# An attention kernel on one core: the next image's v loaded by halves over 26 steps, the sum's halves added first, the output multiplied and stored sooner

## The chip, the core and the metric

The kernel runs on one core of a Trainium2 chip. The metric is the time of one execution on the device in microseconds. Five engines take part: TensorE (PE, with its weight loads shown as PEld), VectorE (DVE), ScalarE (ACT), GpSimd (POOL) and SyncE (SP). Here POOL and SP mostly issue transfers (DMAs). An instruction of an engine, and a transfer of a queue, waits until everything in front of it in the program order of that engine has been issued.

## What is computed

For each of four images of 64 x 64 positions with 256 channels: three projections, attention of all 4096 positions over all 4096, and a residual.

```python
q = jnp.einsum('bwhc,cd->bwhd', x, Wq) + bq
k = jnp.einsum('bwhc,cd->bwhd', x, Wk) + bk
v = jnp.einsum('bwhc,cd->bwhd', x, Wv) + bv
pq, pk, pv = q.reshape(B, -1, N), k.reshape(B, -1, N), v.reshape(B, -1, N)
energy = jnp.einsum('bcn,bcm->bnm', pq, pk)
attention = jax.nn.softmax(energy, axis=-1)
out = jnp.einsum('bcm,bnm->bcn', pv, attention).reshape(B, W, H, C)
return gamma * out + x
```

All is float32. The kernel gets that precision from faster matmuls by splitting each factor into a high part and rests, so that one product is made of three.

## The kernel before

**Steps.** The main loop (line 694) has B * STEPS = 4 * 128 = 512 steps. An image has 8 groups of 512 queries (`g`), a group 16 units of 256 keys (`t`, the unit's number in the group, `n % 16`). Step n does, for each engine in the order written out in the loop: `cross(n + 2)` and `energy(n + 2)` (TensorE: the scores of two steps ahead, lines 369 and 384; ScalarE: a scaling, line 370, and the exponential, line 387), `attend(n, 0)` and `attend(n, 1)` (TensorE: v times the exponentials, line 443, into PSUM banks `a` and `b` that collect over a group), `upper` (ScalarE, line 393) and `halves(n + 1)` (VectorE: adds the exponentials to the group's sum `s`, line 404, and makes the two other parts `l` and `d` of the split, lines 419 and 421, which `attend` of the next step reads).

**The next image's projections** are worked into the steps of the image before (`step`): two blocks of 256 positions per 16 steps, on top of the work above. Their q, k and v parts are stored to DRAM by `store` on SP's queue (line 338). For the last image's steps, from 384 on, there are none.

**Loads on POOL's queue**, in this order within a step: the keys of step n + 5 (`load_k`, line 356; three buffers, so it waits until `energy(n + 2)` has read the buffer), the q of the next group (`load_q`, line 350, in step t = 8), the v of the next image (`load_v`, line 343), and the accumulating load of `finish` (line 502). All of v stands in one tile, `vall[:, t, i]`, whose unit t is overwritten for the next image when the last group of this image is done with it. Before the change unit t of image c is loaded in step 128 c - 13 + t, both halves i in a row, so within 16 steps.

**The end of a group.** In step t = 15, `emptied(n, 0)` (ScalarE, line 463) writes the first half of the result from PSUM into the tile `o`, of which there is one; in step t = 0 of the next group `emptied(n - 1, 1)` writes the other half on VectorE (line 461). Before it may write, the group before must have been stored from `o`. The next group's `attend` needs the emptied banks. `finish` then does the rest of the group in pieces. It is a generator, and `proceed()` at the end of each step runs it to its next `yield`. Counting its pieces from k = 0 at the end of step t = 15, piece k runs in step t = k - 1 of the next group:

- k = 0: the sums `s` (128 x 1024, two halves) are written to DRAM, `zd` (line 469, SP).
- k = 1: they are read back regrouped into `y` (line 474, SP), a tile that shares its buffer with the q of every second group.
- k = 4: both parts of the result are added (line 480, VectorE).
- k = 7: `y` is reduced, transposed, reduced and inverted (lines 483 to 491, VectorE) and written to DRAM, `rd` (line 492, SP).
- k = 8: `rd` is read back to all partitions as `r` (line 495, SP).
- k = 10: the result is multiplied by `r` (line 498, VectorE).
- k = 11: x is added to it by an accumulating load (line 502, POOL).
- k = 14: the result is stored (line 505, SP).

The last group of all goes through `finish_last`, which adds the two halves of the sum in `whole` (line 410) before.

Of the kernel before, what the change touches and what calls it, by code (L numbers as in the profile page):

```python
# [9 lines left out]
F32 = mybir.dt.float32  # L10
# [3 lines left out]
ALU = mybir.AluOpType  # L14
AX = mybir.AxisListType
# [5 lines left out]
def kernel(  # L21
# [36 lines left out]
    nc = tc.nc  # L58
    B, W, H, C = x.shape
    P = 128  # L60
# [21 lines left out]
    NB = 512  # L82
    NJ = NB // P
    NG = N // NB
    NU = NM // 2
    STEPS = NG * NU
# [14 lines left out]
    with ExitStack() as fast:  # L101
# [8 lines left out]
        dram = pool("dram", 2, space=DRAM)  # L110
# [4 lines left out]

        vall = qkv.tile([P, NU, 2, 3, C], F32R, tag="v", name="v")
        wf = qkv.tile([P, 2, 3, KC, C], F32R, tag="wf", name="wf")
        zd = dram.tile([B * NG, 2, P, NB], F32, tag="zd", name="zd", bufs=1)
        rd = dram.tile([B * NG, NB], F32, tag="rd", name="rd", bufs=1)
        xs4 = work.tile([P, 4, 2, XB], F32, tag="o", name="xs", bufs=1)  # L120
        raw = ppool.tile([P, 2, KC, C], F32, tag="x", name="raw")
# [23 lines left out]
        qd, kf, vf, units, loads, now = {}, {}, {}, {}, {}, {}  # L145
# [35 lines left out]
        def image(b):  # L181
            for g in range(NG):
                qd[b, g] = dram.tile([P, NJ, 3, P], F32, tag=f"qd{g}", name=f"qd_{b}_{g}")
            for t in range(NU):
                kf[b, t] = dram.tile([P, 2, 3, P], F32, tag=f"kf{t}", name=f"kf_{b}_{t}")
                vf[b, t] = dram.tile([P, 2, 3, C], F32, tag=f"vf{t}", name=f"vf_{b}_{t}")
# [13 lines left out]
        def load_x(b, i):  # L200
            if b == B or i >= NI:
                return
            if b == 0:
                t = xs4[:, i % 4]
                if i:
                    nc.sync.dma_start(t, xv[b, i])
                loads["x", b, i] = t
                return
            pair = work.tile([P, 2, 2, XB], F32, tag="xd", name=f"x_{b}_{i}", bufs=1)
            for u in range(2):  # L210
                nc.sync.dma_start(pair[:, u], xv[b, i + u])
                loads["x", b, i + u] = pair[:, u]
# [125 lines left out]
                    nc.sync.dma_start(to, f.bitcast(F32))  # L338
            stores.clear()

        def load_v(b, t):
            for i in range(2):
                nc.gpsimd.dma_start(vall[:, t, i], vf[b, t][:, i])  # L343

        def q_tile(g, name, dtype=F32R):
            return work.tile([P, NJ, 3, P], dtype, tag=f"q{g % 2}", name=name, bufs=1)
# [16 lines left out]
        def cross(n):  # L363

            if n >= B * STEPS:
                return
            for i in range(2):
                e = units["e", n, i] = ps_e.tile([P, NB], F32, tag="e", name=f"e_{n}_{i}")
                nc.tensor.matmul(e, *forms(n, i, 2), start=True, stop=False, skip_group_check=True)  # L369
                nc.scalar.mul(e, e, -REST)  # L370
# [25 lines left out]
        def halves(n):  # L396
            if n >= B * STEPS:
                return
            x, h = units[n]

            def summed():
                if n % NU:
                    s = now["s"]
                    nc.vector.tensor_tensor(s, s, x, ALU.add)  # L404
                else:
                    now["s"] = x

            def whole():
                s = now["sum"] = now["s"]
                nc.vector.tensor_tensor(s[:, 0, :], s[:, 0, :], s[:, 1, :], ALU.add)  # L410

            after = 0 < n < 5
            if not after:
                summed()
            if n == B * STEPS - 1:
                whole()
            ld = ppool.tile([P, 2, 2, NB], F32R, tag="ld", name=f"ld_{n}")
            l, d = ld[:, 0], ld[:, 1]
            nc.vector.tensor_tensor(l, x, h.bitcast(F32), ALU.subtract)  # L419

            nc.vector.scalar_tensor_tensor(  # L421
                d, h.bitcast(F32), 1.0 + E, x, ALU.mult, ALU.subtract
            )
            if n == 2:
                next(vs)
                next(vs, None)
            if after:
                summed()
            units[n] = h, l, d
# [35 lines left out]
        def finish(n, o, s):  # L465
            b, g = divmod(n, NG)
            r4 = rall[:, n, :]
            for i in range(2):
                nc.sync.dma_start(zd[n, i], s[:, i, :])
            yield  # L470
            y = q_tile(n, f"y_{n}", F32).rearrange("p j f a -> p (j f) a")
            for j in range(NJ):
                for i in range(2):
                    nc.sync.dma_start(
                        y[j * 32 : (j + 1) * 32, NJ * i : NJ * (i + 1)],
                        zd[n, i].rearrange("(a p) (j c) -> j p a c", p=32, j=NJ)[j],
                    )
            for _ in range(3):
                yield
            nc.vector.tensor_tensor(o[:, 0], o[:, 0], o[:, 1], ALU.add)  # L480
            for _ in range(3):
                yield
            nc.vector.tensor_reduce(
                y[:, 8].rearrange("p (f c) -> p c f", f=NJ),
                y[:, :8].rearrange("p a (c f) -> p c f a", f=NJ),
                AX.X,
                ALU.add,
            )
            nc.vector.transpose(y[:, 9], y[:, 8])
            nc.vector.tensor_reduce(r4, y[:, 9].rearrange("p (f c) -> p f c", f=NJ), AX.X, ALU.add)  # L490
            nc.vector.reciprocal(r4, r4)
            nc.sync.dma_start(rd[n, :].rearrange("(p j) -> p j", j=NJ), r4)
            yield
            r = o[:, 1, 0]
            nc.sync.dma_start(r, rd[n, :].partition_broadcast(P))
            yield
            yield
            nc.vector.tensor_tensor(
                o[:, 0], o[:, 0], r.unsqueeze(1).to_broadcast([P, 2, NB]), ALU.mult
            )  # L500
            yield
            nc.gpsimd.dma_start(o[:, 0], xg[b, g], accum_op=ALU.add)
            for _ in range(3):
                yield
            nc.sync.dma_start(og[b, g], o[:, 0])

        def inside(ok, r):
# [186 lines left out]
        for n in range(B * STEPS):  # L694
            b, u = divmod(n, STEPS)
            g, t = divmod(u, NU)
            final = n == B * STEPS - 1
            if n == 0:
                image(1)
                load_x(1, 0)  # L700
            if u == STEPS - 5 and b + 2 < B:
                image(b + 2)
            if n == B * STEPS - 6:
                xr = ppool.tile([P, 2, NB], F32, tag="s", name="xr")
                nc.sync.dma_start(xr, xg[b, g])
            cross(n + LOOK)
            turn = t == NU - 1 and not final
            if t == 0 and n:
                upper(n + LOOK - 1)
            p = n - 2 + (n > 17)  # L710
            step(p, "act")
            late = n >= (B - 1) * STEPS
            if not final:
                attend(n, 0)
            if late and 1 <= t <= 2 and n > 1:
                emptied(n - 1 - t, 1, done, t - 1)
            energy(n + LOOK)
            load_k(n + LOOK + 3)
            store()
            if t == 0 and n:  # L720
                done = full
            if turn:
                emptied(n, 0)
            else:
                upper(n + LOOK)
            step(p, "pe")
            if turn:
                active.append(finish(n // NU, now["o"], now["s"]))
            if t == 0 and n and not late:
                emptied(n - 1, 1, done, vector=True)  # L730
            halves(n + 1)
            step(p, "dve")
            if final:
                finish_last(n, xr)
                break
            attend(n, 1)
            full = now["a", 1], now["b", 1]
            if n == 17:
                for engine in ("act", "pe", "dve"):
                    step(p + 1, engine)  # L740
            if t == 8 and n + NU < B * STEPS:
                load_q(*divmod(n // NU + 1, NG))
            if n >= STEPS - NU + 3 and (n - 3) // NU % NG == NG - 1 and (n - 3) // STEPS + 1 < B:
                load_v((n - 3) // STEPS + 1, (n - 3) % NU)
            proceed()

    NB = 512
    NG = N // NB
    NJ = NB // P
    NP = NM // 2  # L750
    with tc.If(nc.values_load(again[0:1, 0:1]) > 0), ExitStack() as general:
# [91 lines left out]
        for b in range(B):  # L843
# [16 lines left out]
            for g in range(NG):  # L860
                ps = []
                mx = work.tile([P, 2, NB], F32, tag="mx", name=f"gmx_{b}_{g}")
                for t in range(NP):
# [9 lines left out]
                    p = ppool.tile([P, 2, NB], F32, tag="p", name=f"gp_{b}_{g}_{t}")  # L873
# [52 lines left out]
                r = work.tile([P, NB], F32, tag="r", name=f"gr_{b}_{g}")  # L926
                nc.vector.reciprocal(r, zb)
                for s in range(2):
                    y = work.tile([P, NB], F32, tag="y", name=f"gy_{b}_{g}_{s}")
# [33 lines left out]
```

## Time and profile before

| | |
|---|---|
| median of 3 runs | 2329.9 us (2328.8 to 2330.72) |
| the profiled execution | 2329.92 us |
| its span in the profile | 2328.0 us |
| TensorE's granted clock | 0.999 |

A row of the busy table gives an engine's busy time, its share of the span and the number of instructions. A row of the waits reads "engine line <- what ended the wait: us in total, times, longest us". A row of the chain or of the timeline starts with the start and the duration in us; xN are N instructions merged, and a bracket gives the idle time before and what ended it. A row of instruction groups ends with busy us, mean ns of one, and idle time before. A row of a window gives its length, then busy us of PE, PEld, DVE, ACT and POOL with their counts of instructions, then TensorE's clock, the share of the DMA engines and GB/s. The rows of transfers give the size in KB and the median us from issue to landing; "DMA to landing" gives shortest, median and longest.

### The profile page before, as it was taken

The numbers are of one execution on the slowest core, as the hardware profiler recorded it, in microseconds if no ns is written. First come the engines' busy times: TensorE is split into PE (matmuls) and PEld (weight loads), VectorE is DVE, ScalarE is ACT, GpSimd is POOL, SyncE is SP. The second block draws the span as 40 slices with busy tenths as digits, with TensorE's granted clock in tenths as the row PEclk, the third lists the DMA queues.
The fourth block names the chain that finished last, engine by engine and source line by source line (L and its number), as shares of the span: only waits on it lengthen the run. The fifth ranks groups of instructions, "written<-read, shape, count | busy, mean of one in ns | idle before, by whom it ended". The sixth has DMA issues, their size and how long they took to land.

```text
span 2328.0 us, 31989 instructions
## 1 busy us (share of the span) xinstructions
PE 2309.8 (99%) x10758; PEld 1934.2 (83%) x10758; DVE 2175.0 (93%) x2174; ACT 1797.0 (77%) x2917; POOL 417.3 (18%) x716
## 2 busy tenths in 40 slices
PE   9999999999999999999999999999999999999998
PEld 9888888888878888888888888888887888888887
DVE  8999999999999999999999999999999999888988
ACT  7778777787777777777777777777787788788875
POOL 7111111111321111111132111111113111111110
PEclk9999999999999999999999999999999999999999
DMA  8567765577985776666698567665579745545553
GB/s 266 162 168 210 205 177 155 168 208 200 298 249 167 208 203 180 166 168 195 201 319 246 167 188 206 198 167 167 169 226 332 206 135 142 146 133 149 154 151 97
DMA packets 232190, 445.30 MB, mean 191 GB/s; under 512 B 27986, under 2 KB 109652, under 8 KB 232020
## 3 DMA queue, kind: packets, MB, share of 16 engines
q0 software_dynamic: 101120, 280.54, 45.0%
q1 hardware_dynamic: 130352, 162.38, 20.9%
q8 instruction: 88, 1.44, 0.3%
q14 instruction: 82, 0.67, 0.1%
q10 hardware_dynamic: 548, 0.26, 0.0%
HBM read 321.92 MB, written 120.39 MB: 190 GB/s over the span
## 4 chain that ended last, share of the span: by engine, by line
PE 96%; DMA 3%; ACT 0%; DVE 0%; issue 0%; POOL 0%; ACTq 0%; DVEq 0%
PE a L443 39%; PE e L384 19%; PE b L443 19%; PE e L369 10%; PE qv L257 5%; PE v L274 3%; PE xt L219 1%; DMA out_dram<-o 1%; DMA o<-in_x_dram 1%; DMA k<-kf 1%; DMA rows<-in_L_conv_bk_dram 0%; ACT qv L292 0%; POOL v L343 0%; ACT o L463 0%; POOL k L356 0%
## 5 line engine op out<-in xcount | busy, mean ns | idle before, releaser
L387 ACT ACTIVATE x<-e 128x512 f32<-128x512 f32 x960 | 522.1, 596 | 323.2 <-PE e L384 323.1
L370 ACT ACTIVATE e<-e 128x512 f32<-128x512 f32 x1024 | 546.4, 571 | 135.3 <-PE e L369 135.3
L443 PE MATMUL a<-h,v 128*128 128x512 f32 x2048 | 634.6, 391 | 4.6 <-ACT o L463 4.6
L443 PE MATMUL a<-ld,v 128*128 128x512 f32 x2048 | 631.7, 390 | 0.0
L443 PE MATMUL b<-ld,v 128*128 128x512 f32 x2048 | 631.6, 390 | 0.0
L419 DVE TENSOR_TENSOR ld<-x,h 128x1024 fp32r<-128x1024 f32 x480 | 586.1, 1221 | 37.0 <-ACT h L393 21.0
L404 DVE TENSOR_TENSOR s<-s,x 128x1024 f32<-128x1024 f32 x480 | 585.6, 1220 | 35.2 <-ACT x L387 34.0
L356 POOL DMA_DIRECT2D k<-kf x512 | 272.4, 532 | 1847.9 <-PE e L384 1753.1
L421 DVE SCALAR_TENSOR_TENSOR ld<-h,x 128x1024 fp32r<-128x1024 f32 x480 | 585.6, 1220 | 0.0
L384 PE MATMUL e<-q,k 128*128 128x512 f32 x2048 | 548.1, 390 | 0.0
L393 ACT ACTIVATE h<-x 128x1024 fp32r<-128x1024 f32 x480 | 510.6, 1064 | 14.2
L443 PEld LDWEIGHTS a<-ld,v 128*128 128x128 f32 x2048 | 384.8, 188 | 80.3
L443 PEld LDWEIGHTS b<-ld,v 128*128 128x128 f32 x2048 | 384.7, 188 | 80.0 <-DVE ld L421 0.2
L384 PEld LDWEIGHTS e<-q,k 128*128 128x128 f32 x2048 | 384.6, 188 | 79.4
L443 PEld LDWEIGHTS a<-h,v 128*128 128x128 f32 x2048 | 379.8, 188 | 79.3 <-ACT o L463 5.5
L369 PE MATMUL e<-q,k 128*128 128x512 f32 x1024 | 316.2, 390 | 2.5 <-DMA k<-kf 2.5
L369 PEld LDWEIGHTS e<-q,k 128*128 128x128 f32 x1024 | 191.7, 188 | 43.3 <-ACT o L463 1.8
L310 DVE SCALAR_TENSOR_TENSOR f<-f,qv 128x512 fp32r<-128x512 f32 x128 | 86.1, 683 | 0.3
L419 DVE TENSOR_TENSOR ld<-s,h 128x1024 fp32r<-128x1024 f32 x32 | 39.2, 1226 | 46.6 <-ACT h L393 46.6
L257 PE MATMUL qv<-wf,xf 128*128 128x256 f32 x576 | 78.2, 287 | 0.2
L257 PEld LDWEIGHTS qv<-wf,xf 128*128 128x128 f32 x576 | 74.7, 193 | 3.1 <-issue 0.9
L165 DVE SCALAR_TENSOR_TENSOR vf<-vf,v 128x512 fp32r<-128x512 f32 x96 | 65.4, 682 | 0.5 <-ACT vf L155 0.4
(88 smaller groups left out, 1129.2 us busy)
## 6 DMA issues: line engine op xcount, KB each, us to landing
k<-kf POOLq DMA_DIRECT2D x512, 384.0 KB, 3.6
vf<-vf SPq DMA_DIRECT2D x96, 384.0 KB, 5.2
v<-vf POOLq DMA_DIRECT2D x96, 384.0 KB, 8.3
kf<-f SPq DMA_DIRECT2D x128, 192.0 KB, 3.6
qd<-f SPq DMA_DIRECT2D x124, 192.0 KB, 3.8
q<-qd POOLq DMA_DIRECT2D x31, 768.0 KB, 6.2
zd<-s SPq DMA_DIRECT2D x62, 256.0 KB, 4.9
y<-zd SPq DMA_DIRECT2D x248, 64.0 KB, 4.4
```

What stands on the lines that cost most here:

```text
L257: nc.tensor.matmul(to[:, s, :], left, right.rearrange("p s a -> p (s a)") if w else right, start=(f == 2 and s == k == 0), stop=(f == 1 an ...
L310: nc.vector.scalar_tensor_tensor(f[:, :, :, j, :], h.bitcast(F32), s, y, ALU.mult, op)
L356: nc.gpsimd.dma_start(t, kf[b, u % NU])
L369: nc.tensor.matmul(e, *forms(n, i, 2), start=True, stop=False, skip_group_check=True)
L370: nc.scalar.mul(e, e, -REST)
L384: nc.tensor.matmul(e, *forms(n, i, f), start=False, stop=(f == 1), skip_group_check=True)
L387: nc.scalar.activation(x[:, i, :], e, AF.Exp, scale=(1.0 + E) ** 3 / E)
L393: nc.scalar.activation(h, units[n], AF.Identity, scale=UPPER)
L404: nc.vector.tensor_tensor(s, s, x, ALU.add)
L419: nc.vector.tensor_tensor(l, x, h.bitcast(F32), ALU.subtract)
L421: nc.vector.scalar_tensor_tensor(d, h.bitcast(F32), 1.0 + E, x, ALU.mult, ALU.subtract)
L443: nc.tensor.matmul(to, vall[:, t, i, f, j * P : (j + 1) * P], units[n][f][:, i, :], start=(t == 0 and i == 0 and f != 1), stop=(t == NU - ...
```

## The change

Four parts:

- `load_v` loads one half of a unit. The 32 halves m = 0 to 31 for image c are issued in steps 128 c - 13 + 13 m // 16, so in 26 steps (128 c - 13 to 128 c + 12), one or two halves a step. They reach into the first 13 steps of image c, where unit t is used from step 128 c + t on.
- At the end of each group, not only of the last, `whole` adds the second half of the sum to the first on VectorE, in step t = 14, before `l` and `d` of that step. `zd` gets one half (one write instead of two), `y` is read with four transfers instead of eight, and the first reduction goes over 512 instead of 1024 elements per partition.
- One `yield` less before the multiplication: it and the accumulating load are one unit sooner (k = 9 and k = 10).
- One more `yield` less before the store: it is two units sooner (k = 12).

```diff
-        zd = dram.tile([B * NG, 2, P, NB], F32, tag="zd", name="zd", bufs=1)
+        zd = dram.tile([B * NG, P, NB], F32, tag="zd", name="zd", bufs=1)
...
-        def load_v(b, t):
-            for i in range(2):
-                nc.gpsimd.dma_start(vall[:, t, i], vf[b, t][:, i])
+        def load_v(b, t, i):
+            nc.gpsimd.dma_start(vall[:, t, i], vf[b, t][:, i])
...
-            if n == B * STEPS - 1:
+            if n % NU == NU - 1:
                 whole()
...
-            for i in range(2):
-                nc.sync.dma_start(zd[n, i], s[:, i, :])
+            nc.sync.dma_start(zd[n], s[:, 0, :])
             yield
             y = q_tile(n, f"y_{n}", F32).rearrange("p j f a -> p (j f) a")
             for j in range(NJ):
-                for i in range(2):
-                    nc.sync.dma_start(
-                        y[j * 32 : (j + 1) * 32, NJ * i : NJ * (i + 1)],
-                        zd[n, i].rearrange("(a p) (j c) -> j p a c", p=32, j=NJ)[j],
-                    )
+                nc.sync.dma_start(
+                    y[j * 32 : (j + 1) * 32, :NJ],
+                    zd[n].rearrange("(a p) (j c) -> j p a c", p=32, j=NJ)[j],
+                )
...
             nc.vector.tensor_reduce(
-                y[:, 8].rearrange("p (f c) -> p c f", f=NJ),
-                y[:, :8].rearrange("p a (c f) -> p c f a", f=NJ),
+                y[:, 4].rearrange("p (f c) -> p c f", f=NJ),
+                y[:, :NJ].rearrange("p a (c f) -> p c f a", f=NJ),
                 AX.X,
                 ALU.add,
             )
-            nc.vector.transpose(y[:, 9], y[:, 8])
-            nc.vector.tensor_reduce(r4, y[:, 9].rearrange("p (f c) -> p f c", f=NJ), AX.X, ALU.add)
+            nc.vector.transpose(y[:, 5], y[:, 4])
+            nc.vector.tensor_reduce(r4, y[:, 5].rearrange("p (f c) -> p f c", f=NJ), AX.X, ALU.add)
...
             nc.sync.dma_start(r, rd[n, :].partition_broadcast(P))
             yield
-            yield
             nc.vector.tensor_tensor(
                 o[:, 0], o[:, 0], r.unsqueeze(1).to_broadcast([P, 2, NB]), ALU.mult
             )
             yield
             nc.gpsimd.dma_start(o[:, 0], xg[b, g], accum_op=ALU.add)
-            for _ in range(3):
-                yield
+            yield
+            yield
             nc.sync.dma_start(og[b, g], o[:, 0])
...
-            if n >= STEPS - NU + 3 and (n - 3) // NU % NG == NG - 1 and (n - 3) // STEPS + 1 < B:
-                load_v((n - 3) // STEPS + 1, (n - 3) % NU)
+            for m in range(2 * NU):
+                c, r = divmod(n + NU - 3 - 13 * m // 16, STEPS)
+                if r == 0 and 0 < c < B:
+                    load_v(c, m // 2, m % 2)
             proceed()
```

## Prediction

> **What bounds the kernel now.** I read the busy table first, then the waits, then the chain that ended last, and only then single stretches.
>
> ```profile
> PE 2309.8 (99%) x10758; PEld 1934.2 (83%) x10758; DVE 2175.0 (93%) x2174; ACT 1797.0 (77%) x2917; POOL 417.3 (18%) x716
> ```
>
> The span is 2328.0 us, so TensorE is idle for 18.2 us of it. Something can be gained only inside that idle time, and most of it lies at the start and the end. The waits name what lies between:
>
> ```profile
> ACT o L463 <- DMA out_dram<-o: 5.4, 2, 3.1
> ...
> PE a L443 <- ACT o L463: 4.6, 2, 2.7
> PE e L369 <- DMA k<-kf: 2.5, 3, 1.4
> ```
>
> Two kinds of wait, five events, all where one image passes into the next. In two of them ScalarE (L463) cannot empty PSUM into `o`, because the store of the group before still reads `o`; attend (L443) then waits for the bank. In three, the keys of a coming step land late. The chain of waits shows the first kind around 640 us, and the pace beside it:
>
> ```profile
> 605.00 0.46 PE e L369 x2
> 605.46 0.91 PE a L443 x4
> ...
> 617.74 10.71 DMA o<-in_x_dram
> 628.45 0.02 issue
> 628.47 14.19 DMA out_dram<-o
> 642.66 0.02 issue
> ...
> 643.48 1.20 PE a L443 x4
> ...
> 1793.66 12.15 DMA k<-kf
> 1805.81 0.14 issue
> 1805.95 0.70 PE e L369 x2
> ```
>
> Read the middle lines as a relay: the accumulating load of x took 10.71 us, the store of the result followed it at once and took 14.19, and TensorE stood until it had landed. In the last lines a key load of 12.15 us does the same at the third boundary. Idle time understates the loss, because the first matmuls behind a wait are slower than usual: four cost 1.20 instead of 0.91 (+0.29, twice), two cost 0.70 instead of 0.46 (+0.24, three times). **The loss at the boundaries** is 4.6 + 2.5 + 0.6 + 0.7 = 8.4 us. Some 0.2 more goes in the matmuls that come next, which is an estimate; I take 8.6.
>
> Why are these transfers slow just there? Stretches of 16 us around the first boundary, and the same phases 32 steps (143.6 us) earlier, where no v is loaded (last columns: DMA share, GB/s). The distance is read from the chain, in which the same 16 projections stand 32 steps apart:
>
> ```profile
> 458.07 1.91 PE qv L257 x16
> 601.70 1.91 PE qv L257 x16
> ...
> 616.00:632.00 16.00, 16.00 (x72) 13.29 (x71) 15.50 (x16) 12.91 (x21) 7.57 (x13) 1.00 1.12 343
> 632.00:648.00 16.00, 13.33 (x59) 10.71 (x59) 10.57 (x11) 10.99 (x19) 4.78 (x9) 1.00 1.12 389
> ...
> 472.40:488.40 16.00, 16.00 (x72) 13.26 (x71) 15.48 (x16) 12.89 (x21) 3.28 (x5) 1.00 0.91 270
> 488.40:504.40 16.00, 16.00 (x76) 13.37 (x75) 13.68 (x14) 13.14 (x23) 2.12 (x4) 1.00 0.83 251
> ...
> 552.40:568.40 16.00, 16.00 (x73) 13.25 (x72) 13.47 (x15) 12.57 (x22) 2.12 (x4) 1.00 0.79 257
> ```
>
> The DMA engines are full (share 1.12) at 343 to 389 GB/s. The v loads fill them: the clock stays at 1.00 and nothing else differs. Key loads show the backlog, first from 600 to 660 us, then from 440 to 570 us:
>
> ```profile
> DMA to landing us min/median/max: 3.6/8.6/10.9
> ...
> DMA to landing us min/median/max: 3.3/3.6/5.9
> ```
>
> **The v loads over 26 steps.** The change issues the same 32 halves of 384 KB (0.393 MB) at each boundary, 12.6 MB, two POOL issues per unit as now; what moves is their time.
>
> ```profile
> v<-vf POOLq DMA_DIRECT2D x96, 384.0 KB, 8.3
> ```
>
> Sixteen steps last 71.8 us (half of 143.6), so v now asks for 175 GB/s; over 26 steps (116.7 us) it asks for 108. Added to the rows without v that is 270 + 108 = 378, 251 + 108 = 359 and, in the ten new steps behind the boundary, 257 + 108 = 365 GB/s, where the old demand was 270 + 175 = 445. From the second I take off 33, for half of the sum's write and reads (below). So the demand falls from well above 343 to 389 to just about that. At worst, (378 - 343) x 16 us = 0.56 MB queue up, 1.6 us of work at 343 GB/s; a key load then lands in 3.6 to 5.9 + 1.6, at most 7.5 us. What does it need?
>
> ```profile
> 608.02 0.53 POOL L356 DMA_DIRECT2D k<-kf  x1 [4.42 <-PE e L384]
> ...
> 612.10 0.53 POOL L356 DMA_DIRECT2D k<-kf  x1 [1.68 <-PE e L384]
> ```
>
> Steps without projections are 4.08 us apart; a key load starts 3.02 us into its step (605.00 above) and is used at the start of the third step after it: 3 x 4.08 - 3.02 = 9.2 us. So **the key waits go, 2.5 + 0.7 us**; the bound on the other side is a backlog as large as now, which leaves them (rival 1).
>
> A figure of the Trainium skill speaks against this. Its page DMA: Bandwidth & Descriptors, section Bandwidth, says that the HBM side binds HBM transfers at about 358 GB/s when both cores of a pair stream, and that all issuers share one set of 16 engines. By 358 the slice of 378 still backs up, by an estimated 0.3 MB or 1 us, which is inside the 1.6 above; the row of 389 already carried more than 358, so the row decides.
>
> The queue's new neighbours: POOL runs in order, so each half stands behind that step's key load and before the accumulating load. Instead of two issues a step (some 0.53 us each, like a key load's) there is mostly one, and no added wait: a unit is overwritten at least three steps after its last use, as the step numbers in the code show. The last half, of unit 15, is issued in step 12 of the new image, 3.02 + 0.53 us into it, and used 3 steps later at 0.46: 3 x 4.08 + 0.46 - 3.55 = 9.1 us of cover. Landings with both halves in each step and little else (585 to 600 us):
>
> ```profile
> DMA to landing us min/median/max: 3.8/4.3/4.6
> ```
>
> I take 5 to 7 us: no wait. The upper bound is in rival 4.
>
> **Multiplied, added and stored sooner.** At the boundary the store (L505) was issued in the instant in which the x load had landed (628.45, 628.47), so its place in the program did not hold it; only the multiplication one unit earlier does something there: at least 4.08 us for load and store alike. PE lost 2.67 + 0.29 there and less at the second boundary, so even with landings of 10.71 and 14.19 us this shift alone covers **both store waits, 4.6 + 0.6 us**. Two parts of the change thus cover the same 5.2 us; it counts once. The price is SP: two units sooner, the store waits at the head of SP's queue for the accumulating load, and the stores of q and k forms stand behind it. Usual landings (L502, then L505):
>
> ```profile
> DMA to landing us min/median/max: 6.1/6.5/12.0
> ...
> DMA to landing us min/median/max: 3.0/5.2/14.2
> ...
> 622.24 0.32 SPq L338 DMA_DIRECT2D kf<-f  x1
> ```
>
> The accumulating load now comes one step sooner, behind the key load of 612.10 and one half: 612.10 + 2 x 0.53 = 613.2. With 6.5 to 8 us to landing the store leaves SP at 619.7 to 621.2, before the next one there has its data (622.24). Price nothing; with 10.71 it leaves at 623.9, and the forms' stores wait 1.7 us. Those are needed only in the next image, or by a buffer some steps on.
>
> The multiplication must have `r` one unit sooner. In the group before the boundary:
>
> ```profile
> 603.12 0.34 SPq L495 DMA_DIRECT2D o<-rd  x1
> ...
> 608.95 1.22 DVE L404 TENSOR_TENSOR s<-s,x 128x1024 f32<-128x1024 f32 x1
> ...
> 611.22 1.22 DVE L421 SCALAR_TENSOR_TENSOR ld<-h,x 128x1024 fp32r<-128x1024 f32 x1
> ...
> 614.13 0.41 PEld L443 LDWEIGHTS b<-ld,v 128*128 128x128 f32 x2
> ...
> DMA to landing us min/median/max: 3.9/4.7/6.3
> ```
>
> The new place is 608.95, 5.83 us after `r` was issued; `r` takes 4.7 (last line), at most 6.3, which would hold VectorE 0.47 us. Behind it stands the splitting of the next step, whose L421 ends at 612.44 and is needed at 614.13: 1.69 us of cover, of which the multiplication itself (1.22, as every add of this size) leaves 0.47. Both ends are covered, so I take nothing.
>
> **The halves added first.** VectorE gets one 128x512 add per group, and the regrouping reduces 512 instead of 1024 elements:
>
> ```profile
> L410 DVE TENSOR_TENSOR s<-s 128x512 f32<-128x512 f32 x1 | 0.7, 694 | 0.0
> L483 DVE TENSOR_REDUCE y<-y 128x128 f32<-128x1024 f32 x31 | 61.9, 1995 | 0.0
> ...
> 273.59 1.23 DVE L419 TENSOR_TENSOR ld<-x,h 128x1024 fp32r<-128x1024 f32 x1 [0.80 <-PE e L369]
> ...
> 277.65 1.23 DVE L419 TENSOR_TENSOR ld<-s,h 128x1024 fp32r<-128x1024 f32 x1 [1.10 <-ACT h L393]
> ```
>
> The add costs 0.69 us in the step in which VectorE idles 0.80 and 1.10 us; if that cover were gone it would delay ld by 0.69. The shorter reduction is not in the trace: no saving at one end, half of 1.995 (1.0 us) at the other. I take 1.0, as adds go by length here (1.22 and 0.69). It lets `r` start 1 us sooner and pays for the add. One of two writes of the sum and four of eight reads go: 0.5 MB per group, 33 GB/s in a slice. None is on TensorE's path: nothing.
>
> **Sum**, against the profiled execution: 2329.92 us (span 2328.0 and 1.92 outside), which is the median of the three runs, 2329.9. Minus store waits 5.2, minus key waits 3.2, minus the slow matmuls behind 0.2: 2329.9 - 8.6 = **2321.3 us**. More is not there to gain, as the other idle time stands at the ends.
>
> **Rivals.**
> 1. *The keys take the store's place.* If the backlog stays, key loads wait at the first two boundaries too, 10.9 - 9.2 = 1.7 us each, or 3.2 as at the third. The loss is then 2 x 1.7 + 3.2 = 6.6 to 9.6 where it was 8.4, so 2328 to 2331. For it: key loads between 600 and 660 us took up to 10.9 and were hidden only because TensorE stood. Against it: the v demand falls by 67 GB/s. This is also the case in which the spreading does not do what it says.
> 2. *Only the store waits go*: 2329.9 - 5.2 = 2324.7. For it: the third boundary had no store wait and the longest key loads; against it, the groups behind that boundary have no projections and little other traffic.
> 3. *`r` holds VectorE, slower.* Place: the multiplication, in all 31 groups. `r` may take 5.83 + 0.47 = 6.3 us free; from 6.58 (8.6 / 31 = 0.28 more) the change loses. At 7.3 us it costs 31 x 1.0 = 31, so 2352. For it: 6.3 was seen; against it, the median is 4.7 and the shorter reduction starts it sooner.
> 4. *The last v halves come late, slower.* At the longest landing of keys, 12.15 us, against 9.1, they cost 3.05 us at three boundaries on top of rival 1: 2329.5 + 9.2 = 2339. Against it: one half a step.
>
> **How the numbers follow.** Forecast 78%, with its own range 2319.9 to 2323 (the runs before spread by 1 us each way; 1.5 for a remaining wait). Rival 1 has 8%, rival 2 7%, rival 3 4%, rival 4 3%. A measurement of this kernel tells about 0.2%, 4.7 us, from no change. Faster: the forecast and most of rival 2, 0.83; within: rival 1 and the rest of 2, 0.10; slower: 0.07. The range goes from 2319.9 to 2326.0, to take rival 2 in; about 15% is left out.
>
> **What would show it.** In the changed kernel the waits list should have no L463 on the store and no L369 on keys; key loads around the boundaries should land below 9 us, with a median near 5; v below 8. The reduction should be near 1.0 us; VectorE may wait for `r` some tenths. A wait of TensorE on keys or v in steps 0 to 15 of an image, or of DVE on `o<-rd` above 0.6 us in every group, would make the prediction wrong, and so would a new idle of TensorE in the step of the added half.

## The result, and the profile after

| | before | changed |
|---|---|---|
| median of 12 runs | 2329.9 us | 2324.4 us |
| single executions | 2326.8 to 2330.7 | 2321.6 to 2331.7 |
| the profiled execution | 2329.92 us | 2321.56 us |
| its span | 2328.0 us | 2319.7 us |

The ratio of the times is 0.9981, with a 95% interval from 0.9972 to 0.999. The change makes the kernel faster: by 4.4 us when the ratio is taken (2.3 to 6.5 by its interval), by 5.5 us when the medians are, where 8.6 were forecast. Two things stand out. The profiled execution is almost exactly at the forecast of 2321.3, but it is the fastest of the twelve. And the single executions of the changed kernel spread over 10 us where those of before spread over 4.

The waits of the changed kernel, in which L442, L368, L355 and L462 are the lines that were 443, 369, 356 and 463:

```profile
POOL k L355 <- PE e L383: 1799.5, 497, 5.5
...
ACT vf L155 <- DMA qd<-f: 9.6, 8, 2.4
...
DVE vf L165 <- ACT vf L155: 4.0, 6, 1.0
...
DVE o L494 <- DMA o<-rd: 2.7, 3, 1.3
...
PE e L368 <- ACT x L386: 0.3, 1, 0.3
```

The forecast waits are gone: no row has the emptying of the banks waiting for the store, and none has TensorE waiting for keys. In their place a row has grown that was small before: ScalarE, before the first operation on a v form (L155), waits until a store of an earlier q form (`qd<-f`) has landed and its buffer is free. Before the change the row was

```profile
ACT vf L155 <- DMA qd<-f: 2.7, 5, 0.9
```

The DMA engines around the first boundary, in the columns shown before (DMA share, GB/s):

```profile
616.00:632.00 16.00, 16.00 (x71) 12.86 (x70) 14.33 (x15) 12.13 (x20) 4.15 (x8) 1.00 1.10 355
632.00:648.00 16.00, 16.00 (x75) 12.92 (x74) 14.12 (x15) 13.21 (x23) 4.63 (x9) 1.00 1.08 344
680.00:696.00 16.00, 16.00 (x72) 13.25 (x71) 15.18 (x15) 12.55 (x20) 5.97 (x11) 1.00 1.01 300
```

In the first two of these stretches, 32 us long, they are still full, but the backlog is smaller. The key loads from 600 to 660 us (first line; 3.6/8.6/10.9 before) and all v halves (second; 3.7/8.3/13.9 before) land sooner:

```profile
DMA to landing us min/median/max: 3.3/5.8/8.6
...
DMA to landing us min/median/max: 3.7/5.9/10.2
```

The rows of the transfers show who pays (last number: median us from issue to landing). First two rows of before, then the changed kernel, whose accumulating load took 6.5 before:

```profile
kf<-f SPq DMA_DIRECT2D x128, 192.0 KB, 3.6
qd<-f SPq DMA_DIRECT2D x124, 192.0 KB, 3.8
...
kf<-f SPq DMA_DIRECT2D x128, 192.0 KB, 4.7
qd<-f SPq DMA_DIRECT2D x124, 192.0 KB, 5.4
...
o<-in_x_dram POOLq DMA_DIRECT2D x31, 512.0 KB, 7.5
```

These are medians over all groups, so the collision is not one of the boundaries alone. Away from the boundaries it is not waited for: there the latest landing on record of a first block's stores is 51.4 to 54.9 us into its group, and ScalarE takes the buffer at 55.5. All eight waits stand in the last group of an image or the first of the next, where v loads run too. Where it reaches TensorE can be followed in the timeline of the first steps of the second image (POOL, SP, ScalarE, TensorE):

```profile
684.60 1.15 POOL L498 DMA_DIRECT2D o<-in_x_dram  x1
...
686.12 0.32 SPq L338 DMA_DIRECT2D kf<-f  x1
686.49 0.77 SPq L338 DMA_DIRECT2D qd<-f  x1
687.31 0.97 SPq L338 DMA_DIRECT2D kf<-f  x1
688.32 1.22 SPq L338 DMA_DIRECT2D qd<-f  x1
693.62 0.60 SPq L501 DMA_DIRECT2D out_dram<-o  x1
...
697.85 0.60 ACT L155 ACTIVATE vf<-v 128x512 fp32r<-128x512 f32 x1 [2.38 <-DMA qd<-f]
698.35 1.08 ACT L386 ACTIVATE x<-e 128x512 f32<-128x512 f32 x2
...
698.99 0.99 PE L368 MATMUL e<-q,k 128*128 128x512 f32 x2 [0.32 <-ACT x L386]
```

The accumulating load leaves POOL 1.5 us before the first of the four stores of the first block's q and k forms leaves SP. The chain of waits has the last of them on it, issued at 688.32 and landing 9.42 us later:

```profile
688.32 9.42 DMA qd<-f
697.75 0.02 issue
```

ScalarE stands 2.38 us for it, the exponential behind it is late, the score bank is not free, and TensorE waits. Counted over step lengths (each step's length from the starts of its score matmuls, against the usual length of its place in the group), TensorE loses 1.7 us in this execution, where it lost 8.8 before: 0.5 in steps 125 and 127 ahead of the first boundary, 1.0 in steps 140 and 141 behind it, 0.1 in step 383.

The two rows of the sum, the regrouping's reduction and the added half:

```profile
L480 DVE TENSOR_REDUCE y<-y 128x128 f32<-128x512 f32 x31 | 33.3, 1074 | 0.0
L409 DVE TENSOR_TENSOR s<-s 128x512 f32<-128x512 f32 x32 | 22.2, 692 | 1.1
```

### The profile page after: what moved, and what is told of

Same layout as the page of the kernel before. It is cut to its first block, busy times and chain, and to the rows that moved or that the text cites. A ratio compares the mean times of both kernels' runs of the same rounds, so it can differ in the third digit from the quotient of the medians.

```text
span 2319.7 us, 31772 instructions
## 1 busy us (share of the span) xinstructions
PE 2308.2 (100%) x10758; PEld 1930.9 (83%) x10758; DVE 2169.7 (94%) x2205; ACT 1796.3 (77%) x2917; POOL 416.6 (18%) x716
## 4 chain that ended last, share of the span: by engine, by line
PE 98%; DMA 1%; DVE 0%; ACT 0%; issue 0%; SPq 0%; ACTq 0%; DVEq 0%
PE a L442 40%; PE e L383 20%; PE b L442 20%; PE e L368 10%; PE qv L257 5%; PE v L274 3%; PE xt L219 1%; DMA qd<-f 0%; DMA raw<-in_L_conv_Wk_dram 0%; SPq L338 0%; ACT qv L292 0%; ACT x L386 0%; DVE s L403 0%; DVE xf L165 0%; ACT h L392 0%
## 5 line engine op out<-in xcount | busy, mean ns | idle before, releaser
L442 PE MATMUL a<-h,v 128*128 128x512 f32 x2048 | 633.5, 390 | 0.0
L442 PE MATMUL a<-ld,v 128*128 128x512 f32 x2048 | 631.0, 389 | 0.0
L442 PE MATMUL b<-ld,v 128*128 128x512 f32 x2048 | 630.8, 389 | 0.0
L355 POOL DMA_DIRECT2D k<-kf x512 | 272.5, 532 | 1849.0 <-PE e L383 1799.5
L442 PEld LDWEIGHTS a<-ld,v 128*128 128x128 f32 x2048 | 384.5, 188 | 80.6
L442 PEld LDWEIGHTS b<-ld,v 128*128 128x128 f32 x2048 | 384.3, 188 | 80.3 <-DVE ld L420 0.2
L442 PEld LDWEIGHTS a<-h,v 128*128 128x128 f32 x2048 | 379.7, 188 | 74.1
L368 PE MATMUL e<-q,k 128*128 128x512 f32 x1024 | 316.3, 390 | 0.3 <-ACT x L386 0.3
L368 PEld LDWEIGHTS e<-q,k 128*128 128x128 f32 x1024 | 192.0, 188 | 41.4 <-ACT x L386 1.1
```

The lines of the kernel that those rows point to most:

```text
L355: nc.gpsimd.dma_start(t, kf[b, u % NU])
L442: nc.tensor.matmul(to, vall[:, t, i, f, j * P : (j + 1) * P], units[n][f][:, i, :], start=(t == 0 and i == 0 and f != 1), stop=(t == NU - ...
```

## The experiments

**Theory T**: the accumulating load, one unit sooner, falls among the stores of step t = 10; their buffer comes free late. **Rivals**: V, the v halves in the new steps 131 to 140 do it; S, the store of the result, two units sooner, stands at the head of SP's queue and holds the stores behind it; M, the multiplication one unit sooner disturbs VectorE.

"Loss" below is what TensorE loses by the step lengths of the profiled execution, counted as above. Parts are named A (v spread), B (halves added first), C (multiplication and accumulating load one unit sooner) and D (store one unit sooner still).

**A alone.** The kernel of before with

```diff
-        def load_v(b, t):
-            for i in range(2):
-                nc.gpsimd.dma_start(vall[:, t, i], vf[b, t][:, i])
+        def load_v(b, t, i):
+            nc.gpsimd.dma_start(vall[:, t, i], vf[b, t][:, i])
...
+            for m in range(2 * NU):
+                c, r = divmod(n + NU - 3 - 13 * m // 16, STEPS)
+                if r == 0 and 0 < c < B:
+                    load_v(c, m // 2, m % 2)
```

> Only the v loads spread over 26 steps; sum, multiplication and store as before. Theory T (the accumulating load, one unit sooner, lands among the stores of the first q and k forms in step t = 10, their buffer comes free late, ScalarE waits at the first v form and TensorE behind it): no such collision here, so all boundary waits of 8.4 us go and nothing is added: 2321 to 2323, narrow spread, ScalarE's wait on qd<-f near the 2.7 us of before. Rival V (the v halves in steps 131 to 140 themselves delay the forms' stores): 2324 and a spread of 5 us or more, wait on qd<-f about 9 us. If the store wait at the boundaries needs the sooner multiplication, L463 still waits and the time is 2325 to 2327.

Measured: 2320.0 us (2320.0 to 2322.1, 5 runs), ratio 0.9961 (0.9948 to 0.9975). TensorE loses 0.0 us over all steps, and the wait has gone:

```profile
ACT vf L155 <- DMA qd<-f: 0.2, 1, 0.2
```

So the spread alone takes all the boundary waits, store waits included, and its time lies below that of the whole change (and 1 us below what T expected). V falls.

**B, C and D without A.** The changed kernel with both places of the diff above undone.

> The change without the spread: v loaded in 16 steps as before, sum halved, multiplication and store sooner. The prediction's rival 1 as a kernel: store waits go (covered by one unit), key waits appear at all three boundaries, 6.6 to 9.6 us in all: 2328 to 2331. If the key waits do not appear at the first two boundaries: 2324.7. Theory T adds 1 to 3 us to either and a spread.

Measured: 2333.7 us (2332.2 to 2340.6, 11 runs), ratio 1.0023 (1.0014 to 1.0032), slower than before. No emptying waits for the store, so C and D (beside B) do cover the store waits without A; which of them does was not tried. But neither does TensorE wait for keys. What stands there is the same row as in the changed kernel, larger: 17.5 us in 6 waits over the whole run, and from 615 to 640 us these rows:

```profile
ACT vf L155 <- DMA qd<-f: 4.8, 2, 3.9
...
PE e L369 <- ACT x L387: 1.9, 1, 1.9
```

Step lengths give a loss of 13.7 us, all in steps t = 12 to 15 of the last groups of the first three images. The buffer of the forms is waited for before the key buffers are, although key loads took up to 10.4 us.

**A and B, without C and D.**

```diff
             nc.sync.dma_start(r, rd[n, :].partition_broadcast(P))
             yield
+            yield
...
             nc.gpsimd.dma_start(o[:, 0], xg[b, g], accum_op=ALU.add)
             yield
             yield
+            yield
             nc.sync.dma_start(og[b, g], o[:, 0])
```

> The change with multiplication, accumulating load and store back at k = 10, 11 and 14; v spread and sum halved. Theory T: 2321 to 2322.5, spread below 3 us, wait on qd<-f 3 us or less, no store wait at the boundaries. Rival V: 2324 and the spread of the changed kernel. Rival S (the store at the head of SP's queue delays the forms' stores): also 2321 to 2322.5, so this run does not tell S from T.

Measured: 2321.5 us (2320.3 to 2322.0, 5 runs), ratio 0.9965 (0.9951 to 0.9979), loss 0.0. ScalarE has no wait on `qd<-f` at all. B costs nothing on TensorE, and no step gets shorter either.

**A, B and C; the store at its old place, k = 14.**

```diff
             nc.gpsimd.dma_start(o[:, 0], xg[b, g], accum_op=ALU.add)
             yield
             yield
+            yield
+            yield
             nc.sync.dma_start(og[b, g], o[:, 0])
```

> The change with only the store's place back at k = 14; multiplication and accumulating load stay one unit sooner. Theory T: as the changed kernel, about 2324 with its spread, wait on qd<-f 7 us or more. Rival S: 2321 to 2322.5 and the wait on qd<-f down to 3 us.

Measured: 2322.3 us (2321.7 to 2325.4, 7 runs), ratio 0.997 (0.9959 to 0.9982). The wait stays, as T has it, and all five of its pieces (1.0 to 3.2 us) are at the first v form (t = 12):

```profile
ACT vf L155 <- DMA qd<-f: 8.5, 5, 3.2
```

TensorE loses 2.5 us. The time, however, is in the range that was expected for S (2321 to 2322.5) and not at the 2324 that was expected for T. So C accounts for a part only.

**The multiplication alone sooner** (A and B; multiplication at k = 9, accumulating load at k = 11, store at k = 14).

```diff
             yield
+            yield
             nc.gpsimd.dma_start(o[:, 0], xg[b, g], accum_op=ALU.add)
             yield
             yield
+            yield
             nc.sync.dma_start(og[b, g], o[:, 0])
```

> The change with the multiplication one unit sooner (k = 9) but the accumulating load back at k = 11 and the store at k = 14. Theory T (the accumulating load among the stores of the first forms is what costs): no TensorE loss, 2320 to 2321.5, wait of ScalarE on qd<-f below 1 us, forms' stores of step 10 near 4.1 us to landing. Rival M (the multiplication, in front of the next steps' work on VectorE or held by r, is what costs): 2322 to 2323 as with only the store put back, and the wait on qd<-f stays.

Measured: 2319.4 us (2319.3 to 2321.6, 5 runs), ratio 0.9961 (0.9947 to 0.9975), loss 0.0, no wait of ScalarE on `qd<-f`. This kernel differs from the one before it in the place of the accumulating load alone. The same place in time as above (SP, then POOL) shows the order turned round, stores first and the accumulating load 1.3 us behind the last of them:

```profile
685.22 0.32 SPq L338 DMA_DIRECT2D kf<-f  x1
...
686.60 0.47 SPq L338 DMA_DIRECT2D qd<-f  x1
```

```profile
687.87 1.11 POOL L499 DMA_DIRECT2D o<-in_x_dram  x1
```

Over all groups the stores of t = 10 land after 3.0 us in the median, with the accumulating load one step sooner (the four kernels that have it so) after 6.3 to 6.6. M falls and T is shown: of C, the accumulating load costs and the multiplication does not.

**The store alone sooner** (A and B; multiplication at k = 10, accumulating load at k = 11, store at k = 12).

```diff
             nc.sync.dma_start(r, rd[n, :].partition_broadcast(P))
             yield
+            yield
...
             nc.gpsimd.dma_start(o[:, 0], xg[b, g], accum_op=ALU.add)
             yield
-            yield
             nc.sync.dma_start(og[b, g], o[:, 0])
```

> The change with multiplication and accumulating load back at k = 10 and 11, the store at k = 12, the place that it has in the change. Theory T: the store's place costs little by itself, 2320 to 2322. Rival S (the store at the head of SP's queue waits for the accumulating load and holds the second forms' stores of step t = 12): 2322 to 2324 with a spread of 4 us or more, second forms' stores landing later than 6 us, ScalarE waits at the second v form (t = 14).

Measured: 2324.4 us (2321.4 to 2328.0, 9 runs), ratio 0.9978 (0.9968 to 0.9988), loss 5.3 us. This kernel differs from A and B in the store's place alone. S is right as well, at another place: all four longer waits of ScalarE (1.2 to 3.4 us) are now at the second v form, t = 14, and none at the first. SP's own waits (first the kernel with the multiplication alone sooner, then this one) and the largest case in SP's and ScalarE's timeline:

```profile
SPq L503 <- DMA o<-in_x_dram: 159.0, 9, 20.3
```

```profile
SPq L501 <- DMA o<-in_x_dram: 376.6, 31, 20.4
```

```profile
1273.68 0.60 SPq L501 DMA_DIRECT2D out_dram<-o  x1
1274.39 0.54 SPq L338 DMA_DIRECT2D kf<-f  x1
...
1276.62 0.45 SPq L338 DMA_DIRECT2D qd<-f  x1
...
1283.17 0.60 ACT L155 ACTIVATE vf<-v 128x512 fp32r<-128x512 f32 x1 [3.36 <-DMA qd<-f]
```

The store waits in all 31 groups instead of 9, and the second block's stores leave after it. (The totals hold time in which nothing else was ready for SP, so they are more than the delay.) In the median over groups 1 to 23, the last store of the second block leaves 58.0 us into its group, against 54.7 with A and B. From issue to landing these stores take 4.7 us against 4.2. So they come late because they leave late, and not, as was expected under S, because they land after more than 6 us. The case shown costs TensorE 3.9 us (steps 270 and 271).

**The changed kernel, and A alone, once more.**

> The changed kernel once more, for a second profile and times on the same chip as the others of this call: 2323 to 2326, single executions up to 2330. By theory T its loss lies in steps t = 12 and 13 around the boundaries; whether it grows in the slower executions only their profile can show.

> Only the v loads spread, once more beside the changed kernel: 2319.5 to 2321, single executions within 2.5 us, no loss on TensorE. If it comes out within 1 us of the changed kernel, the first result for it was the chip's.

Measured: the changed kernel 2323.6 us (2321.3 to 2326.8, 11 runs), ratio 0.9973 (0.9964 to 0.9982), a loss of 2.4 us, mostly in t = 12 and 13 at the first two boundaries; A alone 2321.4 us (2319.9 to 2322.3, 5 runs), ratio 0.9963 (0.9949 to 0.9977), loss 0.0, and 2.2 us below the changed kernel beside it. The four runs without the sooner accumulating load and store (A alone twice, A and B, and these with the multiplication sooner) stand between 2319.4 and 2321.5, and their intervals overlap. Their intervals also touch those of the changed kernel, but their single executions hardly do: all 20 lie at 2322.3 or below, and 19 of the 23 of the changed kernel above that. From the start of step 18, behind the first group, to that of step 507 the four profiles agree to a hundredth, 2144.59 us; the changed kernel takes 2146.3 and 2147.0, the kernel of before 2153.4. What else differs between profiled executions stands mostly before step 0, which begins after 64.4 to 67.1 us in the ten profiles, whatever the kernel.

## Why the prediction was right and wrong

- **The figure**: in part luck. The median, 2324.4, is above the forecast's own range (2319.9 to 2323); it lies inside the stated one, up to 2326.0, because that was stretched for rival 2, whose key waits did not stay. The 8.6 us of the sum are outside the interval of the ratio. The one execution at 2321.6 is the fastest, and still has 1.7 us of waits that the prediction does not have.
- **What bounds it**: right. All that was lost lay in the five boundary waits. Counted by step lengths it was 8.8 us against the 8.6 of the sum, and the four runs that lose nothing come out 8.0 to 10.3 us below the runs of before beside them (2329.5 and 2329.7).
- **The v loads**: right in what they take away, a little short in the landings. The key loads between 600 and 660 us landed after 5.8 in the median and 8.6 at most (forecast: near 5, below 9, and 7.5 as the worst of the backlog); one at the second boundary took 9.8. The v halves took up to 10.2 (forecast: 5 to 7, below 8), but none was waited for: the tightest landed 3.1 us before its use. The prediction counted two covers for the store waits; A alone does it, and so does the change without A.
- **The sum's halves**: right. The reduction took 1.07 us (forecast 1.0), the add 0.69, and no step got longer.
- **The multiplication**: right. VectorE waited for `r` three times, 2.7 us in all, the longest 1.3 (the prediction took 0.47 as the most), and with the multiplication alone sooner, where such waits stand too (2.8 us), no loss follows.
- **The accumulating load and the store**: the step that failed. The prediction priced them "nothing", on the ground that the forms' stores "are needed only in the next image, or by a buffer some steps on". The buffer is the point: there are two, the first form's is wanted again two steps after its stores are issued, and those two steps are 7 to 9 us (issued from 686.1 to 688.3 in the timeline above, wanted at 697.85 - 2.38 = 695.5). The prediction counted when the stores would be issued (SP free at 621 us, before 622.24), not how long they take beside the accumulating load, which it had itself put at 613.2, beside the stores of the form before that (613.1 in the timeline of before). The landing of the first block's stores grew from 4.0 to 6.6 us. (That of the second block's grew from 3.0 to 4.8, but it is 4.7 with the multiplication alone sooner too, where nothing is lost.) In the changed kernel's profile both places are waited at: four waits at the first v form, 6.0 us in all, by T, and four at the second, 3.6 us, where S acts, since at the boundaries the accumulating load takes 9.0 to 10.8 us and holds the store at SP's head, as the prediction had it for 10.71.

  Sized by the medians of the runs: the accumulating load sooner 1 to 3 us (2322.3 against 2319.4 to 2321.5), the store sooner by itself 3 to 5 (2324.4), both together 2 to 5 (2324.4 and 2323.6). They need not add: with the accumulating load sooner the store finds it landed sooner, and the second block's last store leaves 55.5 us into its group in the median instead of 58.0.
- **Rival 1** named the wrong buffer. With the backlog left as it was (and C and D beside it), the forms' buffer gave way first, and it cost more (2333.7) than the range of that rival.

What stays open: the changed kernel's slowest executions (2327 to 2332) have no profile. That they are more and longer waits of the same kind is likely, since of all the kernels only ones with those waits spread over 6 us or more, but it was not seen; the time before step 0 can account for under 3 us of it, by the ten profiles.

## What to carry to other kernels

A transfer that is moved sooner is to be checked against every buffer whose release hangs on the transfers that it now meets, not only against what follows it in its own queue; a double buffer that is stored and claimed again after two steps has its slack in the landing time. Where a stall has two possible cures, try each alone: here the spread of the loads was the whole gain, and what was moved along with the second cure gave about a third of it back. And where single executions spread more than before, look for a wait that sits close to its limit.

## What the runs showed of the hardware

Four stores of 192 KB on SP's queue that leave within about 2 us behind an accumulating load of 512 KB on POOL's queue land after 6.3 to 6.6 us in the median, and after 3.0 to 4.1 where they leave before it. The accumulating load takes 7.1 to 7.5 us in the first case and 6.5 to 7.0 in the second. So the transfers hold each other up although two queues issue them. The strided reduction takes 1.9 to 2.1 ns per element and partition (1984 ns for 1024, 1074 for 512), where an add of 1024 takes 1.22 us. And the DMA engines carried up to 389 GB/s over 16 us on this core (632 to 648 us before the change).
